# A graph layer on one core: the second bias in three bf16 rows, chunk features summed in their own block, one-hot rows for three steps at a time

## The chip, the core and the metric

The kernel runs on one core of a Trainium2 chip. The metric is device time in microseconds (us), 542.68 us as the median of three runs (540.83 to 544.07). One execution was profiled: 542.54 us, with a span of 540.8 us from its first to its last recorded instruction. TensorE is called PE below (PEld is its weight load), VectorE DVE, ScalarE ACT, GpSimd POOL, and SyncE, which issues most transfers, SP.

## The reference

A graph has 6250 nodes with 64 features and 206,250 edges sorted by their target, each with 64 features of its own. Every node is normalized, cut at zero, and sent along its edges; the messages are summed by target and go through two dense layers; the result is added to the input.

```python
def _L0_gnn_ref(node_feat, edge_feat, src, dst, W1, b1, W2, b2):
    msg = node_feat[src] + edge_feat
    agg = jax.ops.segment_sum(msg, dst, num_segments=node_feat.shape[0])
    h = jax.nn.relu(agg @ W1 + b1)
    return h @ W2 + b2
h = jnp.maximum(_layernorm(x, axis=-1), 0.0)
x = x + _L0_gnn_ref(h, edge_attr_64, src, dst, W1, b1, W2, b2)
```

All tensors are float32 and the indices int32.

## The kernel before

The sum over edges has two parts, the node features and the edge features, and PE makes both.

**Node features.** The nodes are cut into windows of three targets. For a window, `count` makes a table of how often each source occurs with each of the three targets: for 128 edges, DVE writes one-hot rows of the low seven bits of the source (`hot_lo`, 128 columns) and of target and high bits together (`hot_key`, 148 columns) (L778), PE multiplies the two into PSUM (`pc`, 147 columns, L788), and ACT copies the counts into `ring` as fp32r (L791). Six windows are one step. DVE's two instructions (L778) serve two steps, and each of the two tiles has two buffers. Fourteen steps are a block of 84 windows and 252 nodes; there are 23 blocks, so 322 steps.

When a block's counts are complete, `multiply` multiplies them with the table of node features `h2` (high and low parts side by side) into a PSUM bank `pv`: 49 fp32r products of 252 columns (L808). They are issued in steps 0 to 6 of the block after, 5, 7, 7, 7, 7, 8 and 8 of them (`PRODUCTS`, L999), right after that step's `count`. The ring has three half blocks, so the copies of step 7 need the products of step 6 to be done.

**Edge features.** The nodes are also cut into chunks of 42; `chunk_hot` writes fp32 one-hot rows for a unit of two chunks (DVE, L405), `chunk_sum` multiplies them with the edge features loaded by SP (24 fp32 products into one PSUM tile `bank`, L417), ACT copies the sums (`by_node`, L420) and asks SP for the features of the unit after the next (`load`, L396), and `chunk_place` adds them into the block's bank `pv` at their columns (L433). A block has three units. For block b these stand in block b + 1: one-hots at steps 5, 7, 9, sums at 7, 9, 11 and places at 9, 11, 13 (`SUMS`, `PLACES`, L998). The tile `hot` has two buffers, `feat` two for each chunk of a unit. The last place of a block is followed by one product of ones with zeros (L435), which closes the accumulation. For block 0 the bank is opened early with a product of zeros (L798), and its sums and places stand in block 0 itself. `add_products` adds a finished bank to the node sums `agg` (DVE, L821), for block b at step 4 of block b + 2.

**The last edges** go another way: 18 groups of 1024 edges, for which POOL gathers node features from a table in DRAM onto the loaded edge features (L279), and PE sums them (L462, L474) in pairs of groups whose place among the steps is fixed when the program is built, from estimates of POOL's and of a step's time (`GATHER_US`, `STEP_US`).

**The dense layers** (`mlp_*`) work on blocks of 252 nodes, 25 in all: `ph` = W1 times the sums (fp32, L849), `hid` by ACT with the first bias (L851), then twice (even and odd nodes) a product of a row of ones with the second bias (L856, fp32, one row) and one with W2 (L857), the copy `y` by ACT (L859), the sum with the input by DVE (L864), and the store by SP. `ph`, `po` and several small products share one PSUM buffer. Up to two layers are issued per block, at steps 7 and 10 (`LAYERS`), from block 10 on; what is not ready by then comes after the last step, among the last block's products and sums.

**One-time work** lies between the steps of the first blocks by a list of step numbers (`before`): keys are unpacked in pairs of 128 windows (DVE, PE, ACT), the chunks' targets are turned, and twelve passes of ACT check that the inputs are within the limits of the fast path (`inside`, L743): three at each of the steps 116, 118, 120 and 122. A second path, for inputs outside the limits, is not taken here.

Each engine works through its own instructions in the order in which the program issues them.

Of the kernel before, what the change touches and what calls it, by code (L numbers as in the profile page):

```python
# [88 lines left out]
assert STEPS % 2 == 0  # L89
NC = NS // CN  # L90
# [12 lines left out]
STEP_US = 1.2  # L103
GATHER_US = 2.2
# [9 lines left out]
def gnn_kernel(ctx: ExitStack, tc: tile.TileContext, x, src_t, dst_t, dst_g, edge, w1, b1, w2, b2, out):  # L114
# [50 lines left out]
    firstp_i = small.tile([1, GP * PQ], I32, name="firstp_i")  # L165
# [10 lines left out]
    zerob = small.tile([P, 1], BF16, name="zerob")  # L176
    nc.vector.memset(zerob, 0.0)
# [6 lines left out]
    minus = small.tile([P, P], BF16, name="minus")  # L184
# [38 lines left out]
    row_n = small.tile([1, RC, JQ], F32, name="row_n")  # L223
# [186 lines left out]
    def chunk_sum(u):  # L410
# [8 lines left out]
        by_node[u] = work.tile([P, GB, D], F32, name="by_node")  # L419
# [7 lines left out]
    def chunk_place(u):  # L427
        b, c, n = units[u]
        of = by_node.pop(u)
        unplaced[b] -= 1  # L430
        for i in range(n):
            a = column(b, (c + i) * CN)
            nc.tensor.matmul(pvs[b][0][i * D:(i + 1) * D, a:a + CN], of[:, i, :], select, start=False, stop=False)  # L433
        if pvs[b][1] == HI and unplaced[b] == 0:
            nc.tensor.matmul(pvs[b][0], onesb, zerob.to_broadcast([P, BN]), start=False, stop=True)  # L435
# [21 lines left out]
    def sum_groups(g, hot, tiles):  # L457
# [6 lines left out]
        by_node["h", g] = work.tile([P, GB, D], F32, tag="by_node", name="by_group")  # L464
# [79 lines left out]
    firstp = small.tile([1, GP, PQ], F32, name="firstp")  # L544
# [39 lines left out]
    b2s = consts.tile([1, D], F32, name="b2s")  # L584
    nc.sync.dma_start(b2s, b2.unsqueeze(0))
# [149 lines left out]
    def inside(n):  # L735
        which, k = divmod(n, 2)
        a = (keys[:, 1, :, 0], rel[:, :NC].rearrange("p c q k -> p (c q k)"))[which]
        m = -(-a.shape[1] // CHECKS)
        for i in range(CHECKS):
            of = a[:, i * m:(i + 1) * m]  # L740
            over = late.tile([P, 2 * CQ], BF16, tag="dstq", bufs=2, name="over")[:, :of.shape[1]]
            at = bad[:, 4 + (which * CHECKS + i) * 2 + k:][:, :1]
            nc.scalar.activation(over, of, AF.Sign, scale=-1.0 if k else 1.0,  # L743
                                 bias=edge_w[:, (1, 3 - which)[k]:(2, 4 - which)[k]], accum_out=at)
# [25 lines left out]
    def count(b, s):  # L770

        t = b * BT + s * ST
        if s % 2 == 0:
            hots[:] = [work.tile([P, 2 * ST, P], BF16, name="hot_lo"),
                       work.tile([P, 2 * ST, K + 1], BF16, name="hot_key")]
            for k, (hot, iota_k) in enumerate(zip(hots, (iota_lo, iota_key))):
                m = hot.shape[2] // 2
                nc.vector.tensor_tensor(  # L778
                    hot.rearrange("p t (m o) -> p t m o", o=2),
                    iota_k.rearrange("p (m o) -> p m o", o=2).unsqueeze(1).to_broadcast([P, 2 * ST, m, 2]),  # L780
                    keys[:, k, t:t + 2 * ST, :].unsqueeze(2).to_broadcast([P, 2 * ST, m, 2]), op=OP.is_equal)
                if k and 0 < b * STEPS + s < OPEN:
                    nc.vector.memset(spare, 0.0)
        hot_lo, hot_key = (hot[:, s % 2 * ST:(s % 2 + 1) * ST, :] for hot in hots)
# [10 lines left out]
    def open_pv(b, clear=False):  # L795
        pvs[b] = [ps.tile([P, 512], F32, tag="pv", name="pv")[:, :BN], 0, clear]
        if clear:
            nc.tensor.matmul(pvs[b][0], onesb, zerob.to_broadcast([P, BN]), start=True, stop=False)  # L798

    def multiply(b, upto):  # L800
# [3 lines left out]
        pv, done, clear = pvs[b]  # L804
        a, z = sorted(((2 * b) % 3, (2 * b + 1) % 3))
        of = ring[:, a:z + 1:z - a]
        for h in range(done, upto):
            nc.tensor.matmul(pv.rearrange("p (k n) -> p k n", k=2), h2[:, h, :], of[:, :, h, :],  # L808
                             start=(h == 0 and not clear), stop=(h == HI - 1 and unplaced[b] == 0))
# [26 lines left out]
    xs = {}  # L836

    def residual(b):
        xs[b] = work.tile([NP, 2, D], F32, name="xs", bufs=3)
# [4 lines left out]
    def mlp_hidden(b):  # L844
# [5 lines left out]
        outs[b] = work.tile([HID, BN], F32, name="hid", bufs=1)  # L850
        nc.scalar.activation(outs[b][:, :n], ph[:, :n], AF.Relu, bias=b1s)  # L851

    def mlp_product(b):
        po = ps.tile([P, 2, D], F32, tag="po", name="po", bufs=1)
        for k in range(2):
            nc.tensor.matmul(po[:pairs[b], k, :], ones[0:1, :pairs[b]], b2s, start=True, stop=False)  # L856
            nc.tensor.matmul(po[:pairs[b], k, :], outs[b][:, k:2 * pairs[b]:2], w2s, start=False, stop=True)  # L857
        y = work.tile([NP, 2, D], F32, name="y")
# [77 lines left out]
    def then(k, f):  # L936
# [6 lines left out]
        3: [lambda: place(9, 3), lambda: open_pv(0, True)],  # L943
# [22 lines left out]
        116: [lambda: inside(0)],  # L966
# [246 lines left out]
```

## Time and profile before

| what | value |
|---|---|
| median of three runs | 542.68 us (540.83 to 544.07) |
| profiled execution, its span | 542.54 us, 540.8 us |
| mean granted clock of PE | 0.931 |
| first product of a count (L788) | 40.0 us after the start |
| first product with the node features (L808) | 62.5 us |
| start of the last block's products | 514.8 us |
| closing and opening products (L435, L798) | 22 and 1 |
| waits of ACT's count copies for PE | 75.5 us in 163 |
| L856: records of PE, mean of one | 100 (two for each of 50 products), 303 ns |
| L420: copies of chunk sums by ACT | 69 of 279 ns |
| L851 and L859, `hid` and `y` by ACT | 25 of 466 ns, 25 of 277 ns |
| passes of the checks (L743) | 6 of 834 ns and 6 of 785 ns, each with a read of some 0.2 us |

Matmuls are pipelined: a record on PE lasts longer than the time for which it keeps the next one back, so what an operation costs PE is read from the distance between starts. A line of the page names the source line, the engine, the operation with output and inputs, their shapes, the count, the busy time, the mean duration in ns, and the engine's idle time before with what ended most of it.

### The profile page before, as it was taken

Reading aid. Unit: us, or ns where it says so; the run is one execution under the profiler, and the core shown is the slowest. Engines: PE = TensorE matmul, PEld = TensorE weight load, DVE = VectorE, ACT = ScalarE, POOL = GpSimd, SP = SyncE. Lnnn points to the kernel's source line nnn. Section 1 sums busy time; section 2 is a strip of 40 time slices with the busy share of each in tenths; the row PEclk is TensorE's granted clock in tenths of the full one; section 3 lists DMA queues with packets and bytes.
Section 4 is the critical chain, followed back from the end, with each engine's and each line's share of the span. In section 5 each row is a group of like instructions: output and inputs, shape, how many; then the busy total and the mean of one; then the engine's idle time right before and its main releaser. Section 6 shows DMA issues by size and latency. Waiting matters only on the chain.

```text
span 540.8 us, 17705 instructions
## 1 busy us (share of the span) xinstructions
PE 457.6 (85%) x7459; PEld 399.0 (74%) x7460; DVE 419.5 (78%) x639; ACT 371.5 (69%) x582; POOL 333.9 (62%) x222
## 2 busy tenths in 40 slices
PE   3027868789899988798699899999999999999984
PEld 2025657678778777687598788888888988888872
DVE  4889977789989987789578687787877877898720
ACT  4557796778787779976467667677767767777711
POOL 7776988888885788888888188368748800000000
PEclk9556989999999999899789999999989999999996
DMA  9867412844764655754828468467467455246440
GB/s 228 237 208 214 122 23 36 228 117 114 195 171 111 186 136 110 196 118 86 213 22 211 108 145 207 91 167 206 93 168 182 84 163 160 84 141 187 126 136 19
DMA packets 116300, 77.72 MB, mean 144 GB/s; under 512 B 27030, under 2 KB 114518, under 8 KB 115990
## 3 DMA queue, kind: packets, MB, share of 16 engines
q1 hardware_dynamic: 93586, 66.31, 41.2%
q0 software_dynamic: 22288, 8.68, 12.7%
q10 hardware_dynamic: 340, 1.54, 0.9%
q8 instruction: 60, 0.98, 0.7%
q14 instruction: 26, 0.21, 0.1%
HBM read 72.51 MB, written 3.99 MB: 141 GB/s over the span
## 4 chain that ended last, share of the span: by engine, by line
PE 63%; ACT 9%; POOL 7%; DVE 7%; issue 6%; DMA 5%; SPq 1%; DVEq 0%; POOLq 0%; ACTq 0%
PE pv L808 24%; PE pc L788 18%; PE bank L417 7%; ACT counts L791 6%; POOL pfeat L279 5%; PE po L857 3%; PE po L856 3%; DMA feat<-in_edge 3%; PE ph L849 3%; ACT over L743 2%; DVE hot_key L778 2%; PE pv L433 1%; DVE hot_lo L778 1%; DMA pfeat<-table,src_p 1%; POOL words L279 1%
## 5 line engine op out<-in xcount | busy, mean ns | idle before, releaser
L791 ACT ACTIVATE counts<-pc 128x882 fp32r<-128x882 f32 x322 | 288.8, 917 | 80.7 <-PE pc L788 75.5
L279 POOL DMA_INDIRECT pfeat<-table,src_p x144 | 279.1, 1938 | 78.0 <-issue 38.7
L788 PE MATMUL pc<-hot_key,hot_lo 128*128 128x147 bf16 x1932 | 183.1, 235 | 26.6 <-DVE hot_key L778 13.0
L778 DVE TENSOR_TENSOR hot_lo<-iota_lo,keys 128x1536 bf16<-128x1536 bf16 x161 | 153.7, 954 | 34.5 <-PE pc L788 33.3
L808 PE MATMUL pv<-counts,h 128*128 128x252 f32 x1127 | 175.6, 296 | 3.8 <-ACT counts L791 3.1
L778 DVE TENSOR_TENSOR hot_key<-iota_key,keys 128x1776 bf16<-128x1776 bf16 x161 | 173.4, 1077 | 0.0
L788 PEld LDWEIGHTS <-hot_lo 128*128 128x128 bf16 x1932 | 134.7, 101 | 46.9 <-DVE hot_key L778 13.5
L808 PEld LDWEIGHTS pv<-counts,h 128*128 128x128 f32 x1127 | 146.5, 193 | 7.4 <-ACT counts L791 6.6
L417 PE MATMUL bank<-feat,hot 128*21 128x64 f32 x3288 | 63.2, 226 | 8.0 <-DMA feat<-in_edge 7.0
L405 DVE TENSOR_TENSOR hot<-rel,iota 128x504 f32<-128x504 bf16 (+1 forms) x69 | 46.6, 677 | 29.4 <-PE bank L417 27.4
L417 PEld LDWEIGHTS bank<-feat,hot 128*21 128x21 f32 x3288 | 50.1, 104 | 15.0 <-DMA feat<-in_edge 8.2
L420 ACT ACTIVATE by_node<-bank 128x128 f32<-128x128 f32 (+1 forms) x69 | 19.3, 279 | 17.1 <-PE bank L417 16.2
L279 POOL DMA_INDIRECT words<-packed,first_i x15 | 21.1, 1406 | 4.6 <-issue 3.4
L859 ACT ACTIVATE y<-po 126x128 f32<-126x128 f32 (+2 forms) x25 | 6.9, 277 | 23.8 <-PE po L857 22.7
L856 PE MATMUL po<-b2s,ones 1*126 1x64 f32 (+2 forms) x100 | 22.2, 303 | 1.2 <-ACT hid L851 1.2
L857 PE MATMUL po<-w2s,hid 128*126 128x64 f32 (+2 forms) x100 | 23.1, 314 | 0.0
L433 PE MATMUL pv<-select,by_node 128*64 128x42 f32 x274 | 22.4, 246 | 0.0
L864 DVE TENSOR_TENSOR y<-y,xs 126x128 f32<-126x128 f32 (+2 forms) x25 | 7.2, 290 | 18.1 <-ACT y L859 10.9
L433 PEld LDWEIGHTS pv<-select,by_node 128*64 128x64 f32 x274 | 14.0, 139 | 8.8 <-issue 0.9
L279 POOL DMA_INDIRECT rows<-in_dst_g,row_i x15 | 16.5, 1102 | 6.2 <-ACT inrow L295 2.2
L856 PEld LDWEIGHTS po<-b2s,ones 1*126 1x126 f32 (+2 forms) x100 | 15.2, 190 | 6.4 <-ACT hid L851 2.0
L849 PE MATMUL ph<-sums,w1s 128*128 128x252 f32 (+2 forms) x50 | 17.7, 436 | 1.9 <-ACT sum_p L476 0.8
(195 smaller groups left out, 261.6 us busy)
## 6 DMA issues: line engine op xcount, KB each, us to landing
feat<-in_edge SPq DMA_DIRECT2D x137, 384.0 KB
pfeat<-in_edge SPq DMA_DIRECT2D x72, 64.0 KB
pfeat<-table,src_p POOLq DMA_INDIRECT x144, 4.7
xs<-in_x SPq DMA_DIRECT2D x23, 63.0 KB
out_y<-y SPq DMA_DIRECT2D x23, 63.0 KB
dstn<-in_dst_g SPq DMA_DIRECT2D x1, 1024.0 KB
table<-xl SPq DMA_DIRECT2D x2, 512.0 KB
packed<-dstn ACTq DMA_DIRECT2D x1, 768.0 KB
```

Of the source, the lines that this page charges most:

```text
L279: nc.gpsimd.indirect_dma_start(out=rows, out_offset=None, in_=source, in_offset=bass.IndirectOffsetOnAxis(ap=index, axis=0), compute_op=op)
L405: nc.vector.tensor_tensor(hot_of[u][:, :n].rearrange("p c j w -> p (c j) w"), rel[:, c:c + n].rearrange("p c q k -> p (c q k)").unsqueeze( ...
L417: nc.tensor.matmul(bank[q * QP:q * QP + WQ, i * D:(i + 1) * D], hot[:, i, j, :], feat[i][:, j, :], start=(k == 0), stop=(k == JP - 1))
L420: nc.scalar.activation(by_node[u][:, :n].rearrange("p c d -> p (c d)"), bank[:, :n * D], AF.Copy)
L433: nc.tensor.matmul(pvs[b][0][i * D:(i + 1) * D, a:a + CN], of[:, i, :], select, start=False, stop=False)
L778: nc.vector.tensor_tensor(hot.rearrange("p t (m o) -> p t m o", o=2), iota_k.rearrange("p (m o) -> p m o", o=2).unsqueeze(1).to_broadcast( ...
L788: nc.tensor.matmul(pc[:, k, m * K:(m + 1) * K], hot_lo[:, j, :], hot_key[:, j, :K], start=True, stop=True)
L791: nc.scalar.activation(ring[:, (2 * b + half) % 3, :, i * ST * V:(i + 1) * ST * V].rearrange("p h (k m) -> p h k m", k=2), pc[:, :, :ST // ...
L808: nc.tensor.matmul(pv.rearrange("p (k n) -> p k n", k=2), h2[:, h, :], of[:, :, h, :], start=(h == 0 and not clear), stop=(h == HI - 1 and ...
L849: nc.tensor.matmul(ph[:, :n], w1s, agg[:, start[b]:start[b + 1]], start=True, stop=True)
L856: nc.tensor.matmul(po[:pairs[b], k, :], ones[0:1, :pairs[b]], b2s, start=True, stop=False)
L857: nc.tensor.matmul(po[:pairs[b], k, :], outs[b][:, k:2 * pairs[b]:2], w2s, start=False, stop=True)
```

## The change

- The second bias is held as three bf16 rows whose sum is the fp32 bias (`bias_parts`, ten small DVE instructions at step 104), and is added by a product of three rows of bf16 ones instead of one fp32 row.
- The features of a block's units are summed within the block, at steps 4, 9 and 13 (one-hots two steps earlier), and all three units are placed in the middle of the block's 49 products, at step 3 of the block after. The closing and opening products are gone. The bank is added to the node sums at step 10 of that block.
- One-hot rows are written for three steps per instruction (18 x 128 and 18 x 148 columns instead of 12).
- Layers are issued at steps 8 and 11. The twelve passes of the checks stand one at a time at steps 116, 118 and so on to 138, and what uses them at 142 and 146 instead of 126 and 130.
- To make room, `xs`, `y` and `hid` lie in buffers of tiles used earlier (`words`, `dstq`, `klo`, `khif`, `khi`), some small tiles in pools that are given back, and chunk sums (three buffers) and group sums (one) have tiles of their own.
- The estimates of a step and of a gather are 1.25 and 2.3 us instead of 1.2 and 2.2.

```diff
+R = 3
-STEP_US = 1.2
-GATHER_US = 2.2
+STEP_US = 1.25
+GATHER_US = 2.3
...
-        by_node[u] = work.tile([P, GB, D], F32, name="by_node")
+        by_node[u] = work.tile([P, GB, D], F32, name="by_node", bufs=3)
...
-        if pvs[b][1] == HI and unplaced[b] == 0:
-            nc.tensor.matmul(pvs[b][0], onesb, zerob.to_broadcast([P, BN]), start=False, stop=True)
...
-        by_node["h", g] = work.tile([P, GB, D], F32, tag="by_node", name="by_group")
+        by_node["h", g] = work.tile([P, GB, D], F32, name="by_group", bufs=1)
...
-    b2s = consts.tile([1, D], F32, name="b2s")
-    nc.sync.dma_start(b2s, b2.unsqueeze(0))
+    b2s = consts.tile([3, D], BF16, name="b2s")
+    b2f = small.tile([3, 2, D], F32, name="b2f")
+    nc.sync.dma_start(b2f[:, 0], b2.unsqueeze(0).to_broadcast([3, D]))
+
+    def bias_parts():
+
+        part = small.tile([3, D], BF16, name="b2_part")
+        rows = b2f[:, 1]
+        for k in range(3):
+            nc.vector.tensor_copy(part, b2f[:, 0])
+            nc.vector.tensor_tensor(b2f[:, 0], b2f[:, 0], part, op=OP.subtract)
+            if k == 0:
+                nc.vector.tensor_scalar(rows, part, ident[:3, 0:1], None, op0=OP.mult)
+            else:
+                nc.vector.scalar_tensor_tensor(rows, part, ident[:3, k:k + 1], rows, op0=OP.mult, op1=OP.add)
+        nc.vector.tensor_copy(b2s, rows)
...
     def inside(n):
+        n, i = divmod(n, CHECKS)
         which, k = divmod(n, 2)
...
-        for i in range(CHECKS):
-            of = a[:, i * m:(i + 1) * m]
...
+        of = a[:, i * m:(i + 1) * m]
...
-        if s % 2 == 0:
-            hots[:] = [work.tile([P, 2 * ST, P], BF16, name="hot_lo"),
-                       work.tile([P, 2 * ST, K + 1], BF16, name="hot_key")]
+        r = (b * STEPS + s) % R
+        if r == 0:
+            n = min(R * ST, NW * BT - t)
+            hots[:] = [work.tile([P, R * ST, P], BF16, name="hot_lo"),
+                       work.tile([P, R * ST, K + 1], BF16, name="hot_key")]
...
-        xs[b] = work.tile([NP, 2, D], F32, name="xs", bufs=3)
+        xs[b] = late.tile([NP, 2, D], F32, tag=("words", "dstq")[turns[0] % 2], name="xs", bufs=2)
...
-        outs[b] = work.tile([HID, BN], F32, name="hid", bufs=1)
+        outs[b] = late.tile([HID, BN], F32, tag="khi", name="hid")
...
-            nc.tensor.matmul(po[:pairs[b], k, :], ones[0:1, :pairs[b]], b2s, start=True, stop=False)
+            nc.tensor.matmul(po[:pairs[b], k, :], onesb[:3, :pairs[b]], b2s, start=True, stop=False)
...
-        y = work.tile([NP, 2, D], F32, name="y")
+        y = late.tile([NP, 2, D], F32, tag=("klo", "khif")[turns[0] % 2], name="y")
+        turns[0] += 1
...
-    SUMS, PLACES, LAYERS = (7, 9, 11), (9, 11, 13), (7, 10)
+    SUMS, PLACES, LAYERS = (4, 9, 13), 3, (8, 11)
+    ADDED = 10
...
-        if b == 0:
-            at(5 + 3 * i, chunk_hot, u)
-            at(5 + 3 * i, chunk_sum, u)
-            at(6 + 3 * i, chunk_place, u)
-        elif b < NW - 1:
-            n = first_step[b + 1]
-            places.setdefault(n + PLACES[i], []).append(u)
-            at(n + SUMS[i] - 2, chunk_hot, u)
-            at(n + SUMS[i], chunk_sum, u)
+        n = 5 + 3 * i if b == 0 else first_step[b] + SUMS[i]
+        places.setdefault(b, []).append(u)
+        at(n - 2 if b else n, chunk_hot, u)
+        at(n, chunk_sum, u)
...
-        if b >= 2 and s == 4:
-            add_products(b - 2)
-            if b - 2 > SB:
-                ready.append(b - 2)
         if b >= 1 and s < len(PRODUCTS):
             multiply(b - 1, PRODUCTS[s])
-        for u in places.pop(n, []):
-            chunk_place(u)
-        if b - 2 == SB and 5 <= s < 5 + -(-NX // 4):
-            add_seconds((s - 5) * 4)
-            if s == 4 + -(-NX // 4):
+        if b >= 1 and s == PLACES:
+            for u in places[b - 1]:
+                chunk_place(u)
+        if b >= 1 and s == ADDED:
+            add_products(b - 1)
+            if b - 1 > SB:
+                ready.append(b - 1)
+        if b - 2 == SB and s < -(-NX // 4):
+            add_seconds(s * 4)
+            if s == -(-NX // 4) - 1:
                 ready[:0] = range(SB + 1)
...
     add_sums()
-    add_products(NW - 2)
-    rest = ready + [NW - 2]
-
-    final = [u for u, unit in enumerate(units) if unit[0] == NW - 1]
-    for u in final[:2]:
-        chunk_hot(u)
-    parts = max(2 * len(rest), len(final) + 1) + 2
+    rest = ready
+    parts = 2 * len(rest) + 2
     for k in range(parts):
         multiply(NW - 1, min(HI * (k + 1) // parts, HI - 1))
-        if k < len(final):
-            if k + 2 < len(final):
-                chunk_hot(final[k + 2])
-            chunk_sum(final[k])
-        if 1 <= k <= len(final):
-            chunk_place(final[k - 1])
+        if k == 0:
+            for u in places[NW - 1]:
+                chunk_place(u)
```

More of the change, by code (lines that the diff above doesn't have):

```diff
@@ L738, in inside @@
         m = -(-a.shape[1] // CHECKS)
-        for i in range(CHECKS):
-            of = a[:, i * m:(i + 1) * m]
[L741 to L744, printed above, removed]
+        of = a[:, i * m:(i + 1) * m]
+        over = late.tile([P, 2 * CQ], BF16, tag="dstq", bufs=2, name="over")[:, :of.shape[1]]
+        at = bad[:, 4 + (which * CHECKS + i) * 2 + k:][:, :1]
+        nc.scalar.activation(over, of, AF.Sign, scale=-1.0 if k else 1.0,
+                             bias=edge_w[:, (1, 3 - which)[k]:(2, 4 - which)[k]], accum_out=at)
     def limits():
@@ L793, in count, with open_pv @@
             pc[:, :, :ST // 2 * K].rearrange("p k (m h) -> p h k m", h=HI), AF.Copy)
[L795 to L798, printed above, removed]
+    def open_pv(b):
+        pvs[b] = [ps.tile([P, 512], F32, tag="pv", name="pv")[:, :BN], 0]
     def multiply(b, upto):
@@ L808, in multiply @@
             nc.tensor.matmul(pv.rearrange("p (k n) -> p k n", k=2), h2[:, h, :], of[:, :, h, :],
[L809 removed]
+                             start=(h == 0), stop=(h == HI - 1))
         pvs[b][1] = max(done, upto)
```

42 lines of the change are left out of this document (21 added, 21 removed).

## The prediction

> **What bounds the kernel now.** The span is 540.8 us, the profiled execution 542.54 us; the median of the three runs shown is 542.68 us, so 1.7 us lie outside the span and this execution is an ordinary one. I read the engine totals and slices first.
>
> ```profile
> PE 457.6 (85%) x7459; PEld 399.0 (74%) x7460; DVE 419.5 (78%) x639; ACT 371.5 (69%) x582; POOL 333.9 (62%) x222
> PE   3027868789899988798699899999999999999984
> PEclk9556989999999999899789999999989999999996
> ```
>
> No engine is full over the whole span, but from the middle on PE is. PEclk shows where PE is granted less. Next the costliest groups, for durations:
>
> ```profile
> L791 ACT ACTIVATE counts<-pc 128x882 fp32r<-128x882 f32 x322 | 288.8, 917 | 80.7 <-PE pc L788 75.5
> L778 DVE TENSOR_TENSOR hot_lo<-iota_lo,keys 128x1536 bf16<-128x1536 bf16 x161 | 153.7, 954 | 34.5 <-PE pc L788 33.3
> L778 DVE TENSOR_TENSOR hot_key<-iota_key,keys 128x1776 bf16<-128x1776 bf16 x161 | 173.4, 1077 | 0.0
> ```
>
> 322 steps stand in 23 blocks of 14. The timeline of PE alone gives the block's shape; here one with two output layers (start, us, and at the end the idle time before):
>
> ```profile
> 440.30 0.84 PE L808 MATMUL pv<-counts,h 128*128 128x252 f32 x5
> ...
> 448.93 0.56 PE L788 MATMUL pc<-hot_key,hot_lo 128*128 128x147 bf16 x6
> 449.43 0.87 PE L417 MATMUL bank<-feat,hot 128*21 128x64 f32 x48
> 450.23 0.69 PE L849 MATMUL ph<-sums,w1s 128*128 128x252 f32 x2
> ...
> 452.68 0.43 PE L856 MATMUL po<-b2s,ones 1*126 1x64 f32 x2
> 453.03 0.44 PE L857 MATMUL po<-w2s,hid 128*126 128x64 f32 x2
> ...
> 459.23 0.28 PE L435 MATMUL pv<-zerob,onesb 128*128 128x252 bf16 x1
> 459.35 0.55 PE L788 MATMUL pc<-hot_key,hot_lo 128*128 128x147 bf16 x6
> 460.06 0.85 PE L808 MATMUL pv<-counts,h 128*128 128x252 f32 x5 [0.15 <-ACT counts L791]
> ```
>
> Stretch one (steps 0 to 6: all 49 products of the block before) takes 448.93 - 440.30 = 8.6 us and PE never waits; ACT is busy 6.3 us of it. Stretch two (steps 7 to 13) takes 11.1 us, PE busy 11.05 of 11.2, ACT 8.4. Its end is the first product of the next block, which needs the copy (L791) of step 13. From the same view, starts of products give the blocks' lengths: 19.1, 24.1, 19.4, 19.5, 18.6, 21.4, 19.2, 23.1, 16.7 us for blocks 1 to 9 (no output layer; 181.3 us); 27.1, 21.6, 23.9, 19.8, 21.4, 19.7, 21.2, 21.0, 20.9, 19.8 for 10 to 19 (216.3 us); 18.4, 18.3, 18.0 for 20 to 22 (one layer; 54.7 us); 26.0 us of tail after 514.8. Last, the waits, for what fills the early blocks:
>
> ```profile
> DVE hot L405 <- PE bank L417: 27.4, 19, 1.7
> PE bank L417 <- DMA feat<-in_edge: 7.0, 6, 2.5
> ```
>
> The third one-hot of a block (two buffers) stands in DVE's queue until PE has done the first sum, 27.4 us in 19 times; and feature loads, issued two units ahead within four steps, come late 6 times. After the longest of these (2.52 us, at 264.75) the clock falls (7 and 8 tenths in the slices 257 to 284 us) and stretch one of block 11 takes 10.4 instead of 8.6 us.
>
> **The change, part by part.**
>
> *Bias.* From 452.68 to 453.03 an fp32 bias product holds PE 0.36 us, two per layer. With three bf16 rows it is one pass over 64 columns: the nearest bf16 rows are pc, six in 0.37 us (0.06 each, 147 columns), and the closing product of 252 columns, 0.12 us from its start to the next. I take 0.08 (ends 0.06 and 0.36, the latter if the switch of weights is the price): 0.28 less each, 0.56 per layer, 14 us of PE work over 25 layers. The parts of b2 are ten tiny DVE instructions at step 104, at 0.15 us each 1.5 us, inside DVE's waits for PE there.
>
> [...]
>
> *Closing products (L435) and the opening one (L798).* 22 in the blocks, 0.12 us each: 2.6 us of PE work.
>
> *Sums and places.* Per unit the sum holds PE 0.80 us (449.43 to 450.23) and its places 0.25 us (455.59 to 455.83). Before, all three units lie in stretch two of the block after. Now one sum (step 4) and all three places (step 3) lie in stretch one, where PE is the limit: 8.6 + 0.80 + 0.74 = 10.1 us. Stretch two loses as much PE work, and the question is what is late next there. It is ACT: from the start of step 7, 0.6 us until its copy can begin, 7 x 0.917, one by_node copy 0.28, 0.15 to the product = 7.45 us without a layer; I take 7.6. With layers, hid (0.47) and y (0.28) stand in ACT's queue too, and ph and po share one PSUM buffer, so PE and ACT take turns: counting it through in both queues gives 8.4 to 8.5 us with one layer (PE's sum and second product at step 13 end it) and 8.8 with two (ACT's copy of step 13 ends it); I take 9.0. So a block is 17.7, 18.5 or 19.1 us. Before, undisturbed: 16.7, 18.0 to 18.4, 19.8. Only the third kind gains.
>
> Two things go with it. Chunk one-hots stand at steps 2, 7, 11, with the buffer long free: the 27.4 us of DVE waits end. Units stand 5, 4 and 5 steps apart, so each load has nine steps instead of four: the 7.0 us on feature loads end, and with them the slow clock at 257 to 284 us.
>
> *One-hots of three steps.* From the two forms, (1077 - 954)/(1776 - 1536) = 0.51 ns per element and 167 ns fixed. Three steps: 1.35 + 1.53 = 2.88 us, 0.96 per step against 1.02: 0.055 x 322 = 18 us of DVE work. None is on the path where PE or ACT is the limit, and it is not added. The price: PE waits for a whole group. DVE fills a group while PE takes three steps (3.2 us at ACT's pace), so 2.88 fits, and chunk hots (0.68) eat the group's lead. At the start the first group is 1.0 us longer than 0.87 + 1.00; over block 0, DVE's, 14 x 0.055 = 0.8 us comes back.
>
> *Checks.* Twelve passes of ACT, 0.81 + 0.22 = 1.03 us each. They lay six in stretch one and six in two of block 8; now two and three there and four and three in block 9, so the exposed number stays six. *Product adds* move to step 10 of the same block, four steps after the products end: DVE is not stopped. *xs, hid and y* in the buffers of words, dstq, khi, klo and khif: their last users are at step 138 or before, the first layer at 148. SP and POOL queues keep their order but for the loads, with POOL's first group sum one step later.
>
> **The sum.** Blocks 10 to 19, all with two layers now: 10 x 19.1 + 5 group sums at 0.9 + 0.5 of clock = 196, less 20 against 216.3. Half of that is blocks 10 to 12, where late loads and the slow clock go and block 10 takes a second layer. Blocks 20 to 22: 3 x 18.5 + 0.9 = 56.4, plus 1.7. Blocks 1 to 9: 9 x 17.7 = 159; what stretch one holds over 8.6 us now (9.9 us: unpacking, group sums, turns), plus 1.3 for a moved group and ACT-bound checks, less 1.3 of DVE wait; on ACT in stretch two unpacking, flags and checks 13.5; block 1's clears 1.5: 184, plus 3. Tail: from first product to last now 11.75 us; without three sums, one layer and one set of waits 49 x 0.13 + 0.74 = 7.1, minus 4.6; two layers at the end, one at the low clock, minus 1.5. Together -20 + 1.7 + 3 - 6 = -21: span 519.5, time **521 us**. Its own range is 513 to 528.
>
> **Rivals.** (1) *Early work hides.* The 23 us that I carried over one to one in blocks 1 to 9 partly lie in the other engine's slack (ACT has 3 us in each stretch one, PE 2 us in each stretch two). With the 27.4 us of DVE waits gone, half hides: 521 - 12 = 509. For it: DVE, not PE or ACT, ends most early waits. Against: keys are unpacked by ACT.
>
> (2) *Groups of three bind.* If hots and adds fall between two groups, PE waits 0.4 to 0.7 us in most blocks: 22 x 0.5 = 11, so 532. For it: "PE pc <- DVE hot_key" is already 13.0 us. Against: 18 us less work.
>
> (3) *The second stretch does not shrink.* Slower: stretch one is longer by 1.5 us in 22 blocks (34 us) for certain, and if the ping-pong of ph, hid, po and y through one buffer with the counts copies holds stretch two at its old length less the bias (8.1 and 10.1), blocks 1 to 9 gain nothing (+13.5), the late ones lose 0.5 (+6), the late loads only move (+2), tail -6: 558. It decides from a shortening of stretch two under 34/22 - 6/22 = 1.3 us per block. Against: PE's idle there before is 0.1 us, so its work, not the turns, was the limit with layers.
>
> (4) *The bias stays at 0.36 us*, weights and not passes being the price: 0.56 per layer back where PE ends a stretch, about +7: 528, inside the first case's range.
>
> [...]
>
> **How the numbers follow.** Forecast 0.47, (1) 0.18, (2) 0.15, (3) 0.14, (4) 0.06. The range 506 to 537 leaves out (3) and half of the far ends of (1) and (2). Within 0.5% (540 to 545.4, about what a measurement can tell from no change) lies part of the way from (2) to (3): 0.05; slower 0.13; faster 0.82.
>
> **What would show it.** Right: stretch one 10.1 us, two 9.0 with two layers and ended by ACT's copy; bias to w2 0.08 us; no DVE wait on bank, no PE wait on feature loads; tail near 20 us. Wrong: stretch two above 10 us, or PE waiting for hot_key in most blocks.

## The result, and the profile after

The changed kernel takes 524.0 us (median of 4 runs, 520.68 to 526.25) where the kernel before took 543.33 on the same chip (4 runs, 540.83 to 544.07): a ratio of 0.965 (95% interval 0.958 to 0.972). A later set of six runs gave 0.967 (0.962 to 0.972). The profiled execution took 520.68 us, the least of the four, with a span of 518.9. Medians are of all runs of a kernel, while the ratios leave out three runs that were slower than the others of their kernel (one each of e3 and e6 below and one of the kernel before in the third set below), and the profile of e6 is of such a run.

The engine totals and the slices of PE and of its clock, kernel after:

```profile
PE 437.2 (84%) x7387; PEld 384.5 (74%) x7388; DVE 411.7 (79%) x537; ACT 366.2 (71%) x582; POOL 362.8 (70%) x222
PE   3027689788998998797979999989999999999993
PEclk9556799999999998999979989999999999999996
```

PE has 20 us less work. Its clock still dips from the middle on, in the slices with a 7 at 259 to 272 us and an 8 at 298 to 311: the slow clock that was to go did not. The costliest groups:

```profile
L805 ACT ACTIVATE counts<-pc 128x882 fp32r<-128x882 f32 x322 | 288.0, 918 | 73.6 <-PE pc L802 65.7
...
L792 DVE TENSOR_TENSOR hot_lo<-iota_lo,keys 128x2304 bf16<-128x2304 bf16 x108 | 145.4, 1346 | 40.8 <-PE pc L802 40.4
...
L792 DVE TENSOR_TENSOR hot_key<-iota_key,keys 128x2664 bf16<-128x2664 bf16 x108 | 165.4, 1531 | 0.0
```

The two one-hot instructions take 1346 + 1531 ns for three steps, 16 us less in all than before. Below, the timeline of PE over one block with two output layers, the same one as in the prediction (start, us, and idle time before):

```profile
425.30 0.83 PE L821 MATMUL pv<-counts,h 128*128 128x252 f32 x5
...
430.25 0.55 PE L432 MATMUL pv<-select,by_node 128*64 128x42 f32 x12
430.73 0.57 PE L802 MATMUL pc<-hot_key,hot_lo 128*128 128x147 bf16 x6
...
432.09 0.87 PE L416 MATMUL bank<-feat,hot 128*21 128x64 f32 x48
432.89 0.56 PE L802 MATMUL pc<-hot_key,hot_lo 128*128 128x147 bf16 x6
...
435.70 0.95 PE L802 MATMUL pc<-hot_key,hot_lo 128*128 128x147 bf16 x12
...
438.55 0.57 PE L802 MATMUL pc<-hot_key,hot_lo 128*128 128x147 bf16 x6
439.04 0.24 PE L870 MATMUL po<-b2s,onesb 3*126 3x64 bf16 x1
...
442.87 0.24 PE L870 MATMUL po<-b2s,onesb 3*126 3x64 bf16 x1
443.04 0.45 PE L871 MATMUL po<-w2s,hid 128*126 128x64 f32 x2
443.41 0.24 PE L870 MATMUL po<-b2s,onesb 3*126 3x64 bf16 x1
443.58 0.45 PE L871 MATMUL po<-w2s,hid 128*126 128x64 f32 x2
443.86 0.55 PE L802 MATMUL pc<-hot_key,hot_lo 128*128 128x147 bf16 x6
444.21 0.84 PE L821 MATMUL pv<-counts,h 128*128 128x252 f32 x5
```

All places of a block now stand at once (430.25, 12 records) and hold PE 0.48 us, and one sum stands among the 49 products (432.09, 0.80 us to the next start). Stretch one is 10.4 us here, with 0.26 us for the products that place a group's sums; blocks without these take 10.1. Stretch two runs from 435.70 to 444.21, 8.5 us where it was 11.1. A bias product holds PE 0.17 us (442.87 to 443.04). The waits that answer to those shown before, and two that matter now (total us, times, longest):

```profile
PE pc L802 <- DVE hot_key L792: 12.4, 8, 4.0
...
DVE sums L443 <- PE ph L863: 5.9, 3, 4.4
...
DVE hot L404 <- PE bank L416: 3.4, 2, 3.1
```

DVE's waits for the bank fell from 27.4 us to 3.4, and PE's waits for feature loads (7.0) are gone from the list. The longest wait for one-hot rows, 4.0 us, lies in the opening, ahead of the products with node features. The second line is new: the addition of a group's sums on DVE, held up by a layer's product. From starts of products, as before:

| part of the span | before | predicted | after |
|---|---|---|---|
| to the first product with node features | 62.5 | about the same | 61.7 |
| blocks 1 to 9 | 181.3 | 184 | 179.9 |
| blocks 10 to 19 | 216.3 | 196 | 202.6 |
| blocks 20 to 22 | 54.7 | 56.4 | 54.4 |
| tail | 26.0 | 20 | 20.3 |
| span | 540.8 | 519.5 | 518.9 |

Blocks 10 to 19 take 24.8, 20.7, 19.3, 21.6, 20.9, 18.6, 19.9, 18.6, 19.4 and 18.9 us. The excess over the forecast is mostly in 10, 11 and 13. Here is PE at the end of block 10:

```profile
258.75 0.69 PE L863 MATMUL ph<-sums,w1s 128*128 128x252 f32 x2
259.28 0.55 PE L802 MATMUL pc<-hot_key,hot_lo 128*128 128x147 bf16 x6
262.80 0.56 PE L802 MATMUL pc<-hot_key,hot_lo 128*128 128x147 bf16 x6 [2.96 <-DVE hot_key L792]
```

And DVE at the same time:

```profile
254.42 0.68 DVE L404 TENSOR_TENSOR hot<-rel,iota 128x504 f32<-128x504 bf16 x1
259.48 0.43 DVE L443 TENSOR_TENSOR sums<-sums,sum_p 64x52 f32 x2 [4.38 <-PE ph L863]
259.92 1.36 DVE L792 TENSOR_TENSOR hot_lo<-iota_lo,keys 128x2304 bf16<-128x2304 bf16 x1
261.20 1.54 DVE L792 TENSOR_TENSOR hot_key<-iota_key,keys 128x2664 bf16<-128x2664 bf16 x1
```

DVE stood still for 4.38 us at the group's addition, until the layer's product at 258.75 had read the sums. The next one-hot group was queued behind the addition, so PE had rows for one more step and then waited 2.96 us. In block 13 the chain starts in SP's queue (start, us), and goes on in those of DVE and PE:

```profile
298.22 4.98 SPq L893 DMA_DIRECT2D pfeat<-in_edge  x8
303.25 0.42 SPq L854 DMA_DIRECT2D xs<-in_x  x1
...
303.34 0.43 DVE L443 TENSOR_TENSOR sums<-sums,sum_p 64x52 f32 x2 [1.36 <-PE ph L863]
305.30 0.29 DVE L879 TENSOR_TENSOR y<-y,xs 126x128 f32<-126x128 f32 x1 [1.53 <-DMA xs<-in_x]
...
308.37 0.92 PE L802 MATMUL pc<-hot_key,hot_lo 128*128 128x147 bf16 x6 [1.28 <-DVE hot_key L792]
```

Eight loads of a group's edge features took 4.98 us to issue, and the load of `xs` for a layer stood behind them; DVE's addition of `y` waited 1.53 us for it at 305.3, with a one-hot group behind, and PE waited 1.28 us. The windows of the two stretches one that were slow (of block 11, after the first wait, and of block 13, around the second), and of block 19, undisturbed: the first 10.1 of the 10.4 us of its stretch one, and its stretch two (busy time of PE, PEld, DVE, ACT and POOL, then the granted clock):

```profile
266.40:278.50 12.10, 12.10 (x148) 11.36 (x147) 6.33 (x6) 6.62 (x8) 10.41 (x6) 0.82 0.48 112
306.30:319.40 13.10, 11.82 (x149) 10.96 (x147) 9.92 (x10) 6.75 (x9) 11.37 (x6) 0.87 0.66 167
425.30:435.40 10.10, 10.10 (x150) 9.36 (x148) 7.26 (x9) 6.61 (x10) 0.68 (x1) 1.00 0.49 133
435.70:444.20 8.50, 8.36 (x162) 6.82 (x161) 8.37 (x9) 7.41 (x14) 0.00 (x0) 1.00 0.52 161
```

At granted clocks of 0.82 and 0.87 the stretches took 12.1 and 13.1 us, where an undisturbed one without a group's places takes 10.1 (block 13's holds the 1.28 us wait too). In the undisturbed stretch two PE is busy 8.36 of 8.50 us and ACT 7.41.

### The profile page after: what moved, and what is told of

Same layout as the page of the kernel before. It is cut to its first block, busy times and chain, and to the rows that moved or that the text cites. A ratio compares the mean times of both kernels' runs of the same rounds, so it can differ in the third digit from the quotient of the medians.

```text
span 518.9 us, 17404 instructions
## 1 busy us (share of the span) xinstructions
PE 437.2 (84%) x7387; PEld 384.5 (74%) x7388; DVE 411.7 (79%) x537; ACT 366.2 (71%) x582; POOL 362.8 (70%) x222
## 3 DMA queue, kind: packets, MB, share of 16 engines
q0 software_dynamic: 22288, 8.68, 13.1%
## 4 chain that ended last, share of the span: by engine, by line
PE 58%; DVE 14%; ACT 9%; POOL 8%; DMA 6%; issue 3%; SPq 0%; DVEq 0%; POOLq 0%; ACTq 0%
PE pv L821 22%; PE pc L802 18%; PE bank L416 8%; ACT counts L805 7%; POOL pfeat L278 7%; DVE hot_key L792 4%; DVE hot_lo L792 3%; PE po L871 3%; DMA xl<-in_x 3%; PE pv L432 2%; DMA pfeat<-table,src_p 2%; PE po L870 2%; PE ph L863 1%; PE bank L459 1%; DVE hot L404 1%
## 5 line engine op out<-in xcount | busy, mean ns | idle before, releaser
L278 POOL DMA_INDIRECT pfeat<-table,src_p x144 | 307.9, 2138 | 47.9 <-issue 40.5
L802 PE MATMUL pc<-hot_key,hot_lo 128*128 128x147 bf16 x1932 | 182.6, 234 | 33.8 <-ACT counts L805 14.4
L792 DVE TENSOR_TENSOR hot_lo<-iota_lo,keys 128x2304 bf16<-128x2304 bf16 x108 | 145.4, 1346 | 40.8 <-PE pc L802 40.4
L792 DVE TENSOR_TENSOR hot_key<-iota_key,keys 128x2664 bf16<-128x2664 bf16 x108 | 165.4, 1531 | 0.0
L419 ACT ACTIVATE by_node<-bank 128x128 f32<-128x128 f32 (+1 forms) x69 | 19.6, 284 | 20.3 <-PE bank L416 20.2
L834 DVE TENSOR_TENSOR sums<-sums,pv 128x126 f32<-128x126 f32 (+2 forms) x31 | 10.0, 343 | 13.4 <-PE pv L821 13.3
L863 PE MATMUL ph<-sums,w1s 128*128 128x252 f32 (+2 forms) x50 | 16.4, 410 | 3.1 <-ACT sum_p L473 2.0
L865 ACT ACTIVATE hid<-ph,b1s 128x252 f32<-128x252 f32 (+2 forms) x25 | 11.6, 464 | 9.9 <-PE ph L863 9.9
L871 PEld LDWEIGHTS po<-w2s,hid 128*126 128x126 f32 (+2 forms) x100 | 16.1, 201 | 3.3 <-issue 1.2
L320 PE MATMUL pstart<-begins,first 128*1 128x9 f32 (+1 forms) x30 | 1.3, 172 | 16.8 <-DVE first L298 16.0
```

Of the source, the lines that this page charges most:

```text
L278: nc.gpsimd.indirect_dma_start(out=rows, out_offset=None, in_=source, in_offset=bass.IndirectOffsetOnAxis(ap=index, axis=0), compute_op=op)
L419: nc.scalar.activation(by_node[u][:, :n].rearrange("p c d -> p (c d)"), bank[:, :n * D], AF.Copy)
L792: nc.vector.tensor_tensor(hot[:, :n].rearrange("p t (m o) -> p t m o", o=2), iota_k.rearrange("p (m o) -> p m o", o=2).unsqueeze(1).to_bro ...
L802: nc.tensor.matmul(pc[:, k, m * K:(m + 1) * K], hot_lo[:, j, :], hot_key[:, j, :K], start=True, stop=True)
L863: nc.tensor.matmul(ph[:, :n], w1s, agg[:, start[b]:start[b + 1]], start=True, stop=True)
```

## The experiments

Each ratio is to the kernel before, run beside it on the same chip. The chips differ: the kernel before took 543.59 us in the first set (e8, e4, e1, e2), 551.27 in the second (e6, e7, e3, e5) and 541.52 in the third (the rest), so across sets only ratios are compared. Diffs are to the changed kernel unless said otherwise.

### e8: the bias alone, on the kernel before

```diff
-    b2s = consts.tile([1, D], F32, name="b2s")
+    b2s = consts.tile([3, D], BF16, name="b2s")
...
-            nc.tensor.matmul(po[:pairs[b], k, :], ones[0:1, :pairs[b]], b2s, start=True, stop=False)
+            nc.tensor.matmul(po[:pairs[b], k, :], onesb[:3, :pairs[b]], b2s, start=True, stop=False)
...
+        104: [bias_parts],
```

> The kernel before with the three bf16 bias rows alone. Theory (PE ends stretch two there): a bias product holds PE 0.17 us from its start to the next instead of 0.36, so 50 x 0.19 = 9.5 us of PE work goes, nearly all of it on the path: stretch two with two layers 11.1 to about 10.3 us, time 543 to 534 (532 to 537). Rival A (the price is 0.08 as I predicted): 529. Rival B (ACT and the shared PSUM buffer set stretch two, so only the tail gains): 541.

Measured: 533.62 us, ratio 0.984 (0.977 to 0.990), 10 us less. PE's timeline of this kernel:

```profile
425.53 0.24 PE L871 MATMUL po<-b2s,onesb 3*126 3x64 bf16 x1
425.70 0.45 PE L872 MATMUL po<-w2s,hid 128*126 128x64 f32 x2
426.08 0.24 PE L871 MATMUL po<-b2s,onesb 3*126 3x64 bf16 x1
```

0.17 us to the product with W2, as in the changed kernel and not the predicted 0.08. The undisturbed stretch two with two layers goes from 11.1 to 10.4 us. Fifty products less 0.19 us each are 9.5 us.

### e4: sums and places alone, on the kernel before

The schedule of sums, places, product additions and layers, without closing and opening products; the fp32 bias, rows of two steps and checks in threes stay.

```diff
-    SUMS, PLACES, LAYERS = (7, 9, 11), (9, 11, 13), (7, 10)
+    SUMS, PLACES, LAYERS = (4, 9, 13), 3, (8, 11)
...
+    ADDED = 10
```

> The kernel before with the sums in their own block alone (units summed at steps 4, 9, 13, placed at step 3 of the next block, added at step 10, layers at 8 and 11, no closing product); bias fp32, one-hots for two steps, checks in threes. Theory (this part is most of the gain, through the tail, the late loads and DVE's waits on bank): stretch one 10.1 us, stretch two with two layers about 9.2, no PE wait on feature loads, DVE's wait on bank under 5 us, tail 21.5 us; time 532 (528 to 536). Rival (the sum and the places in stretch one cost what they save, and the one-hots make the gain): 541 or more.

Measured: 531.84 us, 0.981 (0.976 to 0.986), 12 us less. Stretch one is 10.1 us, stretch two with two layers 9.3, and no wait for feature loads is left. Blocks 10 to 19 take 203.7 us, blocks 20 to 22 57.5, which is 2.8 more than before. So the moved sums gain where a block has two layers and lose where it has one; 1.1 to 1.2 us of the loss in each of the last blocks is a wait of PE for rows, which e2 has too and the changed kernel has not.

### e1: the fp32 bias put back

```diff
+    b2r = consts.tile([1, D], F32, name="b2r")
+    nc.sync.dma_start(b2r, b2.unsqueeze(0))
...
-            nc.tensor.matmul(po[:pairs[b], k, :], onesb[:3, :pairs[b]], b2s, start=True, stop=False)
+            nc.tensor.matmul(po[:pairs[b], k, :], ones[0:1, :pairs[b]], b2r, start=True, stop=False)
```

> The changed kernel with the fp32 bias again (bias_parts still runs). Theory (after the other parts PE still ends most of stretch two with two layers): 0.19 x 4 = 0.76 us of PE work per block of two layers comes back, stretch two 8.5 to 9.1 us, tail +1.2: time 524 to 532 (529 to 534). Rival (stretch two is ACT's by now, as I had counted): only the tail and the blocks with one layer, 524 to 526.

Measured: 535.03 us, just above the range expected; 0.983 (0.976 to 0.989) against 0.965 and 0.967 for the changed kernel, which is some 9 us. Stretch two with two layers is 9.3 us instead of 8.5, which is 4 x 0.19 us, all of it on the path. PE ends that stretch, and the rival falls.

### e2: one-hot rows of two steps

```diff
-R = 3
+R = 2
```

> The changed kernel with one-hots for two steps per instruction. Theory (DVE's 18 us of fixed cost lie beside PE and ACT, and a group of three makes single long waits of PE on hot_key): within 3 us of the changed kernel, 521 to 527; PE's waits on hot_key spread, the longest under 2 us instead of 2.96. Rival (fewer DVE instructions make part of the gain): 530 or more.

Measured: 521.85 us, 0.960 (0.955 to 0.965), an interval that overlaps that of the changed kernel. The waits for one-hot rows here:

```profile
PE pc L802 <- DVE hot_key L792: 21.6, 18, 3.8
```

They are more than with three steps and longer in sum (12.4 us in 8 there), and the longest is 3.8 us where under 2 was expected: that part of the expectation missed. But they lie elsewhere. With two steps, blocks 20 to 22 wait 1.1 to 1.2 us each for rows and take 56.2 us (54.4 with three), and blocks 1 to 9 take 188.8, with a 3.85 us wait in block 2 alone. Blocks 10 to 19 take 196.8 instead of 202.6: there a one-hot group stands between the chunk's rows and the group's addition, DVE waits 1.49 us at most at it, and PE's wait of 2.96 us is missing. So the longer groups win time in one place and lose it in another, and the change as a whole gains nothing from them that these runs can tell: the time is inside the range expected, and the rival falls.

### e6 and e7: the additions earlier, or one earlier and one later

e6 has the first edit alone, e7 both.

```diff
-                add_later(n + 6)
+                add_later(n + 4)
...
-        for k, f in ((0, mlp_hidden), (2, mlp_product), (6, mlp_add), (7, mlp_store)):
+        for k, f in ((0, mlp_hidden), (2, mlp_product), (9, mlp_add), (10, mlp_store)):
```

> The changed kernel with the group sums added to the node sums two steps earlier (4 steps after the group's sum instead of 6). Theory (in block 10 the add stands in DVE's queue behind the hidden product of step 11, which reads the same tile, and ahead of the next group of one-hots): DVE's wait for ph of 4.4 us goes, and with it PE's wait for hot_key of 2.96 us and the slow stretch one of block 11 (12.1 instead of 10.1 us): block 10 from 24.8 to about 21.8, 524 to 519 (517 to 522). Rival (DVE then waits for ACT's copy of the group's sum in the same place): 523 to 526, the 2.96 us still there.

> The kernel of e6_group_add_earlier, and the layers' adds of the input three steps later (9 steps after the hidden product instead of 6). Theory (the input's load stands behind eight group loads in SP's queue, DVE waits for it with one-hots behind it, and PE for these): DVE's waits on xs (5.6 us) and y (9.1 us) go, the wait of 1.28 us in block 13 and its slow stretch one (13.1 us) too: 4 us below e6_group_add_earlier, 515 (513 to 518). Rival (slow stretches come of their own and not after a wait): the same as e6_group_add_earlier.

Measured: e6 531.57 us, 0.958 (0.951 to 0.966); e7 532.98 us, 0.964 (0.958 to 0.969). In both the wait of 2.96 us is gone, and block 11's stretch one is back at 10.1 and 10.4 us: its first seven products with node features in a row last 1.07 us in both, against 1.84 in the changed kernel after the wait. But the addition now meets the copy that makes its operand, here in e7:

```profile
DVE sums L443 <- ACT sum_p L473: 5.9, 4, 3.2
```

PE then waits 0.98 us for rows in block 12 and 0.69 in block 14, in both. So a part of the wait was moved and not removed. The price can be read beside e3, which ran on the same chip and still has the wait of 2.96 us: stretch two of block 10 and stretch one of block 11 take 27.0 us together there and 22.3 in e7, while blocks 12 and 14 are 0.5 and 0.9 us longer in e7. The 4 us that e7 was to gain over e6 are not there: on this chip block 13 takes 19.5 us in e6 and e3 too, with no wait of PE for rows over 0.5 us, so the later addition of `y` had nothing to remove. On this chip most blocks took longer in all four kernels for as long as POOL gathered, so their times stand beside each other only.

### e3: the checks in threes again

```diff
-        before.setdefault(116 + 2 * k, []).append(lambda k=k: inside(k))
+        before.setdefault(116 + 2 * (k // CHECKS), []).append(lambda k=k: inside(k))
```

> The changed kernel with the checks in threes again, at steps 116, 118, 120 and 122. Theory (in a stretch one ACT has some 3 us to spare, in a stretch two none, and as many checks lie in stretch two either way; but three in a row keep PE waiting for a free count bank): blocks 8 and 9 from 40.3 to 43 us, time 524 to 527 (525 to 529). Rival (spreading does nothing): 523 to 524.

Measured: 539.68 us, 0.975 (0.966 to 0.985). Blocks 8 and 9, where the passes lie, take 44.7 us together against 41.1 in e6 and 40.9 in e7, but these blocks scatter for other reasons too (43.6 in e1 and 43.4 in e2, with spread passes). Stretch two of block 8 tells the two apart: 13.0 us here, 12.9 to 13.0 in the three other kernels with threes (the kernel before, e4, e8), and 8.9 to 9.2 in all ten with spread passes. About one of these 4 us comes back in stretch two of block 9. PE in block 8 here:

```profile
224.79 0.55 PE L802 MATMUL pc<-hot_key,hot_lo 128*128 128x147 bf16 x6 [1.50 <-ACT counts L805]
...
228.67 0.55 PE L802 MATMUL pc<-hot_key,hot_lo 128*128 128x147 bf16 x6 [1.63 <-ACT counts L805]
...
232.62 1.69 PE L802 MATMUL pc<-hot_key,hot_lo 128*128 128x147 bf16 x12 [2.60 <-ACT counts L805]
```

Three passes in a row hold ACT for 2.2 to 2.4 us (read in the kernel before, where they stand so too: 217.37 to 219.57 and 208.92 to 211.36), its count copy stands behind them and PE runs dry. Spreading them is worth some 3 to 4 us in these blocks. The whole time differs by about as much (0.975 against 0.965 and 0.967), but the intervals overlap.

### e5: the first sum at step 7 in every block

```diff
-    SUMS, PLACES, LAYERS = (4, 9, 13), 3, (8, 11)
+    SUMS, PLACES, LAYERS = (7, 9, 13), 3, (8, 11)
...
-        at(n - 2 if b else n, chunk_hot, u)
+        at(n - (1 if i == 2 else 2) if b else n, chunk_hot, u)
```

> The changed kernel with the first sum at step 7 instead of 4 (the third one-hot at step 12). Theory (stretch one is PE's alone, stretch two ACT's without layers and shared with two): stretch one 10.1 to 9.3 us in all 22 blocks, stretch two longer by 0.3 us without or with one layer and by 0.8 with two: 12 x 0.5 = 6 us less, 518 (516 to 521). Rival A (units at 7, 9 and 13 leave the loads six steps again, and PE waits for features): 524 to 530. Rival B (stretch two is PE's everywhere): 524.

Measured: 536.15 us, 0.969 (0.963 to 0.974), no gain; the forecast of 518 missed. Stretch one is 9.2 us as expected, and blocks 20 to 22 gain 1.5 us (52.9). But stretch two with two layers takes 10.7, 10.3 and 10.3 us in blocks 13, 15 and 17, where e7 on the same chip takes 8.8, 8.9 and 8.5; the sum alone holds PE 0.8. Block 10 takes 30.7 us, 20.8 of them in a stretch two in which the granted clock falls to 5 tenths (slice of 268 to 282 us). Rival A is not shown: of PE's waits at a chunk's sum one of 0.3 us is for a feature load, and 6.3 us in 11 are for nothing that the profile names. In block 19, when POOL has nothing left to gather, it is 9.1 against 8.5 and the whole block is 0.3 us shorter (18.6 to 18.9). What the gathers have to do with the rest was not settled, nor what this edit in every block would give on another chip.

### a2 and e9: the changed kernel again, and both additions later

a2 is the changed kernel. e9:

```diff
-        for k, f in ((0, mlp_hidden), (2, mlp_product), (6, mlp_add), (7, mlp_store)):
+        for k, f in ((0, mlp_hidden), (2, mlp_product), (9, mlp_add), (10, mlp_store)):
...
-                add_later(n + 6)
+                add_later(n + 8)
```

> The changed kernel itself, beside the three that follow, as their reference on the same chip: 0.965 of the kernel before (0.958 to 0.972).

> The changed kernel with the group sums added two steps later (8 after the group's sum, past the next group of one-hots) and the layers' adds of the input three steps later. Theory (what DVE waits for with one-hots behind it costs PE 2.96 us in block 10 and 1.28 us in block 13, and each is followed by a slow stretch one, 2.0 and 3.0 us longer): no wait of PE for hot_key over 1 us in blocks 10 to 19, these blocks together 6 us shorter, 0.954 of before (0.948 to 0.960). Rival (slow stretches come by themselves, the waits only move as they did with the add two steps earlier): 0.962 to 0.966.

Measured: a2 522.22 us, 0.967 (0.962 to 0.972), with the same 2.96 us wait in block 10; e9 513.74 us, 0.951 (0.946 to 0.956), as expected. DVE in e9, where block 10 ends and block 11 begins:

```profile
259.70 1.36 DVE L792 TENSOR_TENSOR hot_lo<-iota_lo,keys 128x2304 bf16<-128x2304 bf16 x1 [0.93 <-PE pc L802]
260.98 1.54 DVE L792 TENSOR_TENSOR hot_key<-iota_key,keys 128x2664 bf16<-128x2664 bf16 x1
263.17 0.43 DVE L443 TENSOR_TENSOR sums<-sums,sum_p 64x52 f32 x2 [0.65 <-PE ph L863]
263.63 1.36 DVE L792 TENSOR_TENSOR hot_lo<-iota_lo,keys 128x2304 bf16<-128x2304 bf16 x1
```

The addition waits for the same product, but a one-hot group has been written first, the wait is 0.65 us, and PE does not notice. The windows of the stretches one and two that follow, in e9:

```profile
266.09:276.17 10.08, 10.08 (x149) 9.44 (x147) 7.57 (x9) 6.72 (x9) 8.86 (x5) 1.00 0.54 138
276.17:284.70 8.53, 8.39 (x162) 6.84 (x161) 8.33 (x10) 7.41 (x14) 7.31 (x5) 1.00 0.76 179
```

The granted clock is 1.00 and the block takes 18.6 us instead of 20.7. Blocks 10 to 19 take 194.1 us, 7.5 less than in a2 (201.6): 3.9 and 2.2 less in blocks 10 and 11, behind the group's addition, and 1.8 less in block 13, behind that of `y`. The medians are 8.5 us apart. The two profiled spans are only 5.2 us apart, since the start, blocks 1 to 9 and the tail were 2.3 us longer in this execution of e9.

### e10 and e11: the first sum at step 7 in blocks without two layers, and with e9

e10 has this edit on the changed kernel; e11 has it and those of e9.

```diff
+        sums = (7 if b < 10 or b > 19 else SUMS[0], *SUMS[1:])
-        n = 5 + 3 * i if b == 0 else first_step[b] + SUMS[i]
+        n = 5 + 3 * i if b == 0 else first_step[b] + sums[i]
...
-        at(n - 2 if b else n, chunk_hot, u)
+        at(n - (1 if i == 2 and sums[0] == 7 else 2) if b else n, chunk_hot, u)
```

> The changed kernel with the first sum at step 7 in the blocks without layers or with one (1 to 9 and 20 to 22), at step 4 in the others. Theory (there stretch two is ACT's and has room on PE; with two layers it has none): stretch one 9.2 us and stretch two longer by 0.3 in 12 blocks, 5 us less, 0.956 of before (0.950 to 0.962). Rival (sums six steps apart bring late loads or DVE waits back): 0.965 or more.

> Both of the two kernels before it. Theory: the gains add, 0.945 of the kernel before (0.938 to 0.953). Rival (one of them does nothing): 0.955 or more.

Measured: e10 520.3 us, 0.961 (0.956 to 0.965), a smaller gain than the 0.956 expected, inside its range: blocks 20 to 22 gain 1.6 us (52.8), but block 2 now has waits of 3.75, 2.04 and 1.13 us, and blocks 1 to 9 gain nothing (182.1). Block 13's wait for rows grew to 2.85 us. e11: 512.04 us, 0.946 (0.942 to 0.949), as expected the best of all, 10 us under the changed kernel on the same chip; most of that is e9's, and its interval meets e9's.

## Why the prediction was right, and where it was not

**The shape held.** Stretch one came out at 10.1 us to the tenth, stretch two with two layers shrank by 2.6 us where rival (3) needed less than 1.3, DVE's waits for the bank fell to 3.4 us and PE's for loads ended, and the tail is 20.3 us. Done alone, the bias gives 10 us and the sums 12 (e8, e4). Spreading the checks gives some 3 to 4 in its blocks, which the prediction counted at nothing ("the exposed number stays six"): that step failed, as three passes in a row hold up the copy behind them (e3). The three-step rows give nothing that can be told. The changed estimates of a step and of a gather were not changed alone; e8 and e4 have the old ones. By their ratios, 0.984 and 0.981, the bias and the sums alone make up the 0.965 measured together, so, as far as the intervals can tell, what the checks add is given back somewhere; the next point is a place where it is.

**The step that failed: "DVE is not stopped", and SP's queue.** It was said of the product additions alone, and even these stop DVE (1.3 to 1.8 us four times in blocks, 6.0 in the tail), without a wait of PE for rows over 0.5 us behind them. The group's addition and that of `y`, moved with the layers to other places in DVE's queue, were not followed there at all: each waits, with a one-hot group behind it. Of SP the text said that the queues keep their order but for the loads, and nothing of how long eight group loads hold back `xs`. So the waits that end (27.4 us of DVE, 7.0 of PE) were replaced by two, and blocks 10 to 19 took 202.6 us, not 196. e9 took both away and gave 194.1; e2, where the rows of two steps leave neither long, gave 196.8. The slow clock of the late blocks, forecast to go, stayed with these waits and went with them: in e9 no slice of the clock after 231 us but the last reads under 9 tenths.

**Bias: mis-sized.** 0.17 us, not 0.08, so 0.19 saved and not 0.28: 9.5 us of PE work instead of 14. It lies inside the ends of 0.06 and 0.36. The 0.08 was the author's estimate from two other bf16 products (0.06 and 0.12 us); what makes the bias product dearer was not shown. Rival (4) fell: 0.36 did not stay.

**Places: mis-sized.** 0.48 us for three units, not 0.74, where three times the 0.25 of one unit was taken: in one row they cost less. The 10.1 us came out all the same, by luck in this term: the 49 products, which the places and the sum now break up, hold PE 6.6 us from start to start where they held 6.4.

**Stretch two: engine and size.** With two layers it is 8.5 us, not 9.0, and PE ends it and not ACT's copy of step 13 (PE busy 8.36 of 8.50; e1 lengthens it by what it adds to PE). With one layer and no group it is 7.5 to 7.8, not 8.4 to 8.5, and PE waits there for ACT (0.61 and 0.25 us in blocks 20 and 22). Counting the turns of both engines gave ACT too much. That made blocks 20 to 22 come out at 54.4 us instead of 56.4.

**Blocks 1 to 9** took 179.9 us (181.2 in a2, 182.6 in e9), not 184. Over 9 x 10.1 us, stretches one held 12.0 us more, where some 10 were counted; over 9 x 7.6, stretches two held 8.5 more, where 15 were. So a part of the carried work hid in stretch two, as rival (1) says, and none in stretch one; at 172 it had too much hidden. **Rival (2)** fell in its form, waits in most blocks; there are two in blocks 10 to 22 over 1 us, at a price of some 8 us (e9) where it named 11 for all. That the forecast of the span is so close, 519.5 us to 518.9, is luck: the early and last blocks were 6 us too long in it and the late ones 6.6 us too short.

## What to carry to other kernels

Split a block into stretches by the engine that ends each, and move work from a full stretch into one where another engine has slack; the gain is then the shrinkage of the one less the growth of the other, per kind of block (here 2.6 us less in a stretch two with two layers, 1.5 us more in stretch one). Then walk the in-order queues of the engines that feed the full one: an addition that waits, or a load behind eight others, delays what is queued behind it (here 4.38 us of wait on DVE became 2.96 us on PE, and 4.98 us of issues on SP were followed by 1.28 us). Such an addition was better late than early here, as nothing needed its result yet: two steps earlier the group's addition waited up to 3.2 us for its operand (e7), two steps later 0.65 us at the end of block 10 (e9).

## What the runs showed of the hardware

- **A long wait was paid twice.** Five kernels have the wait of PE at the end of block 10 (2.96 us in the changed kernel, a2, e1 and e3, 2.99 in e10). In all five the next stretch one took 11.9 to 12.3 us instead of 10.1 (12.1 at a granted clock of 0.82 in the changed kernel), and its first seven products with node features in a row lasted 1.84 us; in the six kernels without a wait over 1.4 us there (e2, e4, e6, e7, e9, e11) it took 10.1 to 10.4 us and these products 1.07 to 1.08 (e9: at a clock of 1.00). In windows of 2 us after the wait the changed kernel's clock reads 0.81, 0.50, 0.50, 0.50, 0.98 and 1.00. Shorter waits were not alike: one of 1.28 us stood in a stretch at 0.87, but 1.06 and 0.51 us in the same block of a2 in one at 1.00, and 2.35 us in block 5 of e2 was followed by seven products in 1.07 us. In the kernel before the clock reads 0.50 from 264.7 to 271 us, after waits of 1.06 and 2.52 us (261.69 and 264.75). What length of wait the clock answers to was not shown.
- **A small bf16 product between fp32 ones was not cheap**: 0.17 us for 64 columns, against 0.06 for each of six bf16 products of 147 columns in a row. A change of type is not the whole reason: six products of a count hold PE 0.49 us when the bias product follows (438.55 to 439.04, both bf16), and 0.35 when a product with the node features does (443.86 to 444.21). Whether it is the load of 126 columns or the three rows was not tried.
- **Longer instructions on DVE went with longer gathers on POOL.** The mean gather took 1.94 and 1.99 us in the kernel before and in e2, with rows of two steps, and 2.10 to 2.20 in nine kernels with three (the changed kernel, a2, e3, e5 to e7, e9 to e11). e2 differs from the changed kernel in this alone (1.99 against 2.14). Why was not tried, and the profiler's spans on POOL are rough.
- **One chip differed in one phase**: 551.27 us against 541.52 and 543.59 for the kernel before. With the changed kernel's variants most blocks up to 18 were longer there while POOL gathered (block 12 is 20.5 us in e3 and 21.0 in e7, 19.3 in the changed kernel elsewhere), and the last ones equal (54.4 us for blocks 20 to 22). The gathers themselves were not longer (2.11 us in e7, 2.14 in the changed kernel). But PE stood still there 10 to 18 times after 63 us, 3.9 to 8.1 us in all, for nothing that the profile names, and in the ten kernels profiled elsewhere once at most, for 0.8 us. That is a part of the difference; its cause stays open.
